# Half-size products for the values and queries of a two-layer graph network, and four moved steps in its projection stage

## The chip, the core and the metric

The kernel runs on one core of a Trainium2 chip. The metric is the device time of one execution in microseconds (us), as the median of several runs. A core has five engines, each with its own in-order queue of instructions: TensorE (in the profile PE, its weight loads PEld), VectorE (DVE), ScalarE (ACT), GpSimd (POOL) and SyncE (SP), which here only starts DMA transfers. [...]

## The reference

Two layers work on x (4096x512) and a weighted adjacency matrix adj (4096x4096), all in float32.

```python
# layer 0
h = jnp.maximum(_layernorm(x, axis=-1), 0.0)
q = h @ Wq.T + bq;  k = h @ Wk.T + bk;  v = h @ Wv.T + bv
a = q @ k.T * scale + adj + adj            # scale = 1/sqrt(512)
x = x + softmax(a, axis=-1) @ v
# layer 1: 8 heads of 64
h = jnp.maximum(_layernorm(x, axis=-1), 0.0)
nX = (h @ W).reshape(n, 8, 64).transpose(1, 0, 2)
nX = a_ln * (nX - mean) / (std + EPS) + b_ln
kg = leaky_relu(at1 + at2.transpose(0, 2, 1), 0.2) * adj    # at1, at2: nX with a1, a2
attention = softmax(where(adj != 0, kg, NEG_FILL), axis=-1)
x = x + elu(attention @ nX + nX)
```

## The kernel before, in words

`fast_path` has three stages. The projection stage (about the first 268 us) makes the values v and the queries; the attention of layer 0 follows, and from about 2100 us on the attention of layer 1. A `general_path` is taken only if a check at the end fails.

**What the projections compute.** Keys are not formed. The two weight matrices are multiplied into one, `a_sb` (Wq and Wk; four groups of matmuls, L662, copied out of PSUM by ScalarE at L666), and `queries` multiplies it with the hidden rows h; the scores are then products of these queries with h itself. `c_sb` holds what the bias bq adds. `half_scale` is half of 1/sqrt(512).

**Rounds.** The 4096 rows of x go in 8 rounds (`sb`, 0 to 7) of 512 rows, 4 tiles of 128. Each round has these parts:

- `load_x`: four DMA transfers of 256 KB on SP's queue (L548), into one of two buffers.
- `normalize`: statistics of the rows on VectorE (L172, L173), the inverse root of the variance (the power at L159 on GpSimd, the rest on VectorE, L161 to L164), then four operations on VectorE that normalize the rows (L557). It runs at the start of the round ahead of the one that uses it.
- `hidden`: 16 transposes on TensorE (L567) into two PSUM buffers, four relu operations of ScalarE (L568) that write the hidden tile `hT`, then four sums and differences of its quarters on GpSimd (L576 to L579, `hS`). Both are stored to HBM on SP's queue (L582).
- `values_of`: for each of the 4 tiles 4 matmuls of 512 columns into one PSUM buffer of four (`pv`, L588), then one addition of the bias on VectorE (L592), which writes into v.
- `queries`: for each of 4 output blocks 4 matmuls of 512 columns into the same four buffers (`pq`, L602), then one operation on VectorE (L606) that adds c_sb, multiplies by half_scale and puts the columns in another order (`sources_of_rows`) in `qs`. `qs` is stored (L610), GpSimd makes four differences of its quarters (L619 to L622), and these are stored with four transfers (L624).

The order of a round `sb` is: normalize(sb+1), load_x(sb+2), values_of(sb), hidden(sb+1), center_weights in round 2 or weigh_weights in rounds 3 to 6, queries(sb).

**Seven products.** The layer-0 attention (`stage`, L733) already multiplies the hidden rows with the queries in halves: both operands are cut into 2x2 blocks, and seven half-size products of sums of blocks (S1 to S4 and T1 to T4) stand in place of eight. That is what `hS` and the differences of the queries are for. An addition on VectorE (L741) takes each partial result out of PSUM.

**Side work.** `attention_vectors` loads small weights of layer 1 on ScalarE's queue and prepares them on VectorE (L194 to L220). `center_weights` (L230 to L232) takes the mean of each head from W on VectorE. `weigh_weights` multiplies W by the attention vectors on GpSimd (L237) and sums on VectorE (L238).

**The start.** x, Wv, then Wq and Wk in blocks (L472) are loaded on SP's queue. normalize(0), hidden(0), loads of bv and bq on ScalarE's queue (L648, L649), transposes of Wq and Wk in 32x32 blocks on VectorE (L478), values_of(0), normalize(1), attention_vectors, the products of Wq and Wk, c_sb, load_x(2), hidden(1), queries(0) follow, and then round 1.

**What sets the order.** The tile framework derives the semaphores from the data. `seq` holds instructions on each engine's queue in the order of the source, so an instruction that waits holds up all that stand behind it on its engine.

Of the kernel before, what the change touches and what calls it, by code (L numbers as in the profile page):

```python
# [78 lines left out]
def fast_path(  # L79
# [153 lines left out]

    def weigh_weights(k):
        for e in range(2):
            t = prep.tile([P, NH, HD], F32, name="prod", tag="prod", bufs=2)
            seq(nc.gpsimd.tensor_mul(t, w1_sb[:, k], aa[e]))  # L237
            seq(nc.vector.tensor_reduce(w1a_sb[:, k, e, :], t, AX.X, ALU.add))  # L238
# [223 lines left out]
    with tc.tile_pool(name="early", bufs=2) as early, tc.tile_pool(name="kv", bufs=1) as kv:  # L462
# [69 lines left out]
        with tc.tile_pool(name="proj_c", bufs=1) as pc, tc.tile_pool(  # L532
# [10 lines left out]
            bv_sb = early.tile([P, D], F32, name="bv_sb", tag="qt", bufs=16)  # L543
# [7 lines left out]
            def normalize(xt):  # L551
                mv = means(work, [xt[:, b, :] for b in range(SB)], "h")
                var = work.tile([P, SB], F32, name="hv", tag="hv", bufs=1)
                seq(nc.vector.tensor_scalar_add(var, mv[:, :, 1], LN_EPS))
                rstd = inverse_root(nc.vector, work, var, SB, "h")
                for b in range(SB):
                    seq(nc.vector.tensor_scalar(  # L557
                        xt[:, b, :], xt[:, b, :], mv[:, b, 0:1], rstd[:, b : b + 1],
                        ALU.subtract, ALU.mult,
                    ))  # L560
# [22 lines left out]

            def values_of(sb):
                for b in range(SB):
                    pv = psum.tile([P, 512], F32, name="pv", tag="mm", bufs=4)
                    for k in range(KC):
                        seq(nc.tensor.matmul(  # L588
                            pv, hidden_of[sb][0][:, k, ts(b, P)], wv_sb[k],
                            start=k == 0, stop=k == KC - 1,  # L590
                        ))
                    seq(nc.vector.tensor_add(v[:, sb * SB + b, :], pv, bv_sb))  # L592
# [3 lines left out]

            def queries(sb):
                qs = pc.tile([P, KC, GC], F32, name="qs", tag="qs", bufs=1)
                for o in range(KC):
                    pq = psum.tile([P, 512], F32, name="pq", tag="mm", bufs=4)  # L600
                    for k in range(KC):
                        seq(nc.tensor.matmul(  # L602
                            pq, a_sb[:, k, ts(o, P)], hidden_of[sb][0][:, k, :],
                            start=k == 0, stop=k == KC - 1,
                        ))
                    seq(nc.vector.tensor_scalar(  # L606
                        sources_of_rows(qs[:, o, :]), pq.rearrange("p (c q r) -> p c q r", c=SB, r=R),
                        c_sb[:, o : o + 1], half_scale, ALU.add, ALU.mult,
                    ))
# [36 lines left out]
            normalize(xts[0])  # L646
# [12 lines left out]
            for k in range(KC):  # L659
                pa_ps = psum.tile([P, 512], F32, name="pa", tag="mm", bufs=4)  # L660
# [929 lines left out]
```

## Time and profile before

| what | us |
|---|---|
| median of 3 runs | 3963.34 (3960.78 to 3963.43) |
| the profiled execution | 3960.13 |
| its span, first to last instruction | 3958.2 |
| TensorE busy in the span | 3786.1 (96%) |
| VectorE, ScalarE, GpSimd busy | 2889.7, 1796.8, 2569.7 |
| first matmul of values_of(1) to that of values_of(7) | 61.2 to 240.5 |
| last matmul of queries(7) ends, about | 268.1 |

The profile is of one execution on the chip. A row of the timeline gives a start, a duration, the engine, the line, the operation, the output and the inputs by their names, and how many instructions were merged into the row; a bracket tells the idle time of the engine before it and what ended it. [...] Each float32 matmul of the source is recorded as two instructions. A row of a line's list gives shortest, median and longest duration in nanoseconds. A wait row gives the time in total, how often, and the longest.

### The profile page before, as it was taken

The numbers are of one execution on the slowest core, as the hardware profiler recorded it, in microseconds if no ns is written. First come the engines' busy times: TensorE is split into PE (matmuls) and PEld (weight loads), VectorE is DVE, ScalarE is ACT, GpSimd is POOL, SyncE is SP. The second block draws the span as 40 slices with busy tenths as digits, with TensorE's granted clock in tenths as the row PEclk, the third lists the DMA queues.
The fourth block names the chain that finished last, engine by engine and source line by source line (L and its number), as shares of the span: only waits on it lengthen the run. The fifth ranks groups of instructions, "written<-read, shape, count | busy, mean of one in ns | idle before, by whom it ended". The sixth has DMA issues, their size and how long they took to land. (4 is left out here: it accounts for less than half of the span.)

```text
span 3958.2 us, 44075 instructions
## 1 busy us (share of the span) xinstructions
PE 3786.1 (96%) x15370; PEld 1788.6 (45%) x15370; DVE 2889.7 (73%) x4331; ACT 1796.8 (45%) x1581; POOL 2569.7 (65%) x1305
## 2 busy tenths in 40 slices
PE   8989999999999999999998899999999999999997
PEld 4446666666666666666652222222222222222222
DVE  5435556565565656556557899999999999999996
ACT  1000111111111111111115788888888888888886
POOL 3432225243242525234257999999999999999998
PEclk9999999999999999999998999999999999999999
DMA  6466657667675766768557544444444444444442
GB/s 214 169 213 195 198 175 207 199 194 213 182 220 161 223 182 191 215 183 223 164 158 190 149 141 141 145 146 138 140 138 145 140 146 146 146 139 146 129 151 79
DMA packets 554407, 670.37 MB, mean 169 GB/s; under 512 B 79808, under 2 KB 397504, under 8 KB 534720
## 3 DMA queue, kind: packets, MB, share of 16 engines
q1 hardware_dynamic: 552112, 665.70, 56.5%
q8 instruction: 122, 2.00, 0.2%
q10 hardware_dynamic: 2064, 1.77, 0.2%
q14 instruction: 109, 0.89, 0.1%
HBM read 495.12 MB, written 172.23 MB: 169 GB/s over the span
## 5 line engine op out<-in xcount | busy, mean ns | idle before, releaser
L999 POOL TENSOR_TENSOR t<-t,g 128x1536 f32<-128x1536 f32 (+1 forms) x512 | 1722.8, 3410 | 34.3 <-DVE t L992 29.1
L1015 PE MATMUL acc<-t,nX 128*64 128x512 f32 x4096 | 994.5, 606 | 66.8 <-ACT t L1002 54.5
L751 POOL TENSOR_TENSOR total<-total,aT 128x512 f32<-128x512 f32 x248 | 340.3, 1372 | 1061.3 <-ACT aT L746 1051.1
L1002 ACT ACTIVATE t<-t 128x2048 f32<-128x2048 f32 x512 | 975.9, 1906 | 85.8 <-POOL t L999 84.6
L761 PE MATMUL acc<-v,aT 128*128 128x512 f32 x2048 | 961.9, 592 | 0.0
L746 ACT ACTIVATE aT<-aT 128x512 f32<-128x512 f32 x256 | 161.2, 630 | 1322.8 <-DVE aT L741 1314.8
L992 DVE TENSOR_TENSOR t<-t,d 128x1024 f32<-128x1024 f32 x512 | 619.9, 1211 | 12.3 <-ACT t L976 12.3
L976 ACT ACTIVATE t<-d 128x1024 f32<-128x1024 f32 x512 | 524.8, 1025 | 227.7 <-PE d L969 205.0
L969 PE MATMUL d<-nb,ident_b 128*128 128x512 bf16 x2048 | 536.3, 385 | 1.5 <-DMA nb<-nT_d 1.5
L1015 PEld LDWEIGHTS acc<-t,nX 128*64 128x64 f32 x4096 | 250.4, 136 | 595.3 <-issue 340.1
L761 PEld LDWEIGHTS acc<-v,aT 128*128 128x128 f32 x2048 | 389.7, 190 | 272.4 <-issue 244.9
L986 DVE SCALAR_TENSOR_TENSOR d<-u,at2m,d 128x512 f32<-128x512 f32 x542 | 407.0, 751 | 50.1 <-PE d L969 35.2
L741 DVE TENSOR_TENSOR aT<-aT,X 128x256 f32<-128x256 f32 x512 | 214.9, 420 | 280.5 <-PE X L733 277.3
L986 DVE SCALAR_TENSOR_TENSOR t<-u,at2m,d 128x512 f32<-128x512 f32 x482 | 360.0, 747 | 49.2 <-DVE d L986 0.9
L741 DVE TENSOR_TENSOR aT<-aT,Z 128x256 f32<-128x256 f32 x384 | 159.6, 416 | 292.3 <-PE Z L733 287.6
L991 DVE TENSOR_TENSOR t<-d,g 128x512 f32<-128x512 f32 (+1 forms) x512 | 366.0, 715 | 5.1 <-DMA g<-gT_d 1.8
L725 DVE SCALAR_TENSOR_TENSOR gs<-ng,aT 128x512 f32<-128x512 bf16 x256 | 285.8, 1117 | 10.1 <-DMA gT_d<-gs 1.4
L964 PE MATMUL d<-z,z 6*128 6x512 bf16 x2048 | 250.1, 385 | 35.2 <-DVE t L991 15.4
L964 PEld LDWEIGHTS <-z 6*128 6x128 bf16 x2048 | 76.4, 91 | 443.2 <-issue 439.1
L733 PE MATMUL Z<-qt,hS 128*128 128x256 f32 x1024 | 265.7, 382 | 9.0 <-DVE aT L741 8.3
L969 PEld LDWEIGHTS <-ident_b 128*128 128x128 bf16 x2048 | 159.2, 98 | 241.6 <-issue 121.9
L733 PE MATMUL X<-qt,hS 128*128 128x256 f32 x1024 | 263.8, 380 | 0.0
(170 smaller groups left out, 3124.9 us busy)
## 6 DMA issues: line engine op xcount, KB each, us to landing
g<-gT_d SPq DMA_DIRECT2D x128, 1024.0 KB, 5.5
ag<-in_adj_dram SPq DMA_DIRECT2D x256, 256.0 KB, 5.7
hT<-h_d SPq DMA_DIRECT2D x64, 1024.0 KB, 5.9
hS<-s_d SPq DMA_DIRECT2D x64, 1024.0 KB, 8.3
gT_d<-gs SPq DMA_DIRECT2D x256, 256.0 KB, 3.0
nb<-nT_d SPq DMA_DIRECT2D x128, 512.0 KB, 5.1
nT_d<-ng SPq DMA_DIRECT2D x256, 128.0 KB, 3.4
z<-z_d SPq DMA_DIRECT2D x143, 128.0 KB, 4.7
```

Of the source, the lines that this page charges most:

```text
L733: seq(nc.tensor.matmul(out, a, b, start=start and k == 0, stop=k == 1, skip_group_check=not start,))
L741: seq(nc.vector.tensor_add(p, p, part))
L751: seq(nc.gpsimd.tensor_add(totals[ic], totals[ic], p))
L761: seq(nc.tensor.matmul(sums[ic][b], probs[s][:, ts(b, P)], v[:, jt, :], start=jt == 0, stop=jt == NB - 1))
L969: seq(nc.tensor.matmul(pair[hh // 2][:, hh % 2, :], ident_b, ng[:, jt % JB, :], start=False, stop=True))
L976: seq(nc.scalar.activation(t[:, 0:2, :], zs[n][0], AF.Relu, scale=4.0))
L986: seq(nc.vector.scalar_tensor_tensor(pair[1][:, e, :] if e > 1 - mine else t[:, 2, :], u4[:, e, :], at2m[:, jt, h : h + 1], pair[1][:, e, ...
L991: seq(nc.vector.tensor_mul(t[:, HG - mine : HG, :], pair[1][:, 2 - mine : 2, :], g))
L992: seq(nc.vector.tensor_add(t[:, 0:2, :], t[:, 0:2, :], pair[0]))
L999: seq(nc.gpsimd.tensor_mul(t[:, 0:mine, :], t[:, 0:mine, :], g))
L1002: seq(nc.scalar.activation(logits[n], logits[n], AF.Exp))
L1015: seq(nc.tensor.matmul(grp["acc"][hf][ts(e, HD), :], nX[jt // SB][:, jt % SB, hg * HG + 2 * hf + e, :], t[:, 2 * hf + e, :], start=jt == 0 ...
```

## The change

`values_of` and `queries` are computed with the seven-product scheme. A new function `seven` runs the products in four steps over two lanes; a lane is a pair of row tiles for the values, and a pair of output blocks for the queries. It has two PSUM buffers X and two Z, one of each per lane, of 256 columns. After each product, `take` moves the partial sum out on VectorE: the first into an output block adds the bias (or c_sb), the others add to what is there. Sums of blocks of Wv (`sum_wv`) and of a_sb (`sum_a`) are made once on GpSimd. half_scale goes into a_sb and c_sb. bv_sb has a buffer of its own, and `pa` has two PSUM buffers for four.

`normalize` is split. `deviations_of` makes the statistics on VectorE and the inverse root on GpSimd, with a shift, two rounds ahead; the new `normalize` applies both on ScalarE at the end of the round. `weigh_weights` keeps only GpSimd's products, and `sum_weighed` sums them on VectorE one round later. `center_weights` moves behind `queries`. A round is now: load_x(sb+2), values_of(sb), hidden(sb+1), deviations_of(sb+2), sum_weighed, queries(sb), center_weights or weigh_weights, normalize(sb+2).

```diff
@@ -231,11 +231,16 @@
         seq(nc.vector.tensor_scalar_mul(m, m, 1.0 / HD))
         seq(nc.vector.tensor_sub(w1_sb, w1_sb, m.unsqueeze(3).to_broadcast([P, KC, NH, HD])))
 
+    weighed = {}
     def weigh_weights(k):
         for e in range(2):
-            t = prep.tile([P, NH, HD], F32, name="prod", tag="prod", bufs=2)
-            seq(nc.gpsimd.tensor_mul(t, w1_sb[:, k], aa[e]))
-            seq(nc.vector.tensor_reduce(w1a_sb[:, k, e, :], t, AX.X, ALU.add))
+            weighed[k, e] = prep.tile([P, NH, HD], F32, name="prod", tag="prod", bufs=2)
+            seq(nc.gpsimd.tensor_mul(weighed[k, e], w1_sb[:, k], aa[e]))
+    def sum_weighed(k):
+        for e in range(2):
+            seq(nc.vector.tensor_reduce(w1a_sb[:, k, e, :], weighed.pop((k, e)), AX.X, ALU.add))
 
     def make_ready(ic, x1s, small, at_step, gap, last):
 
@@ -540,7 +545,12 @@
             ]
             a_sb = pc.tile([P, KC, D], F32, name="a_sb")
             c_sb = pc.tile([P, KC], F32, name="c_sb")
-            bv_sb = early.tile([P, D], F32, name="bv_sb", tag="qt", bufs=16)
+            bv_sb = pc.tile([P, D], F32, name="bv_sb")
+            wv_sums, a_sums = [
+                [early.tile([P, KC // 2, H], F32, name=name, tag="qt", bufs=16) for _ in range(4)]
+                for name in ("wvs", "as")
+            ]
 
 ...
-            def normalize(xt):
+            def deviations_of(xt):
                 mv = means(work, [xt[:, b, :] for b in range(SB)], "h")
                 var = work.tile([P, SB], F32, name="hv", tag="hv", bufs=1)
-                seq(nc.vector.tensor_scalar_add(var, mv[:, :, 1], LN_EPS))
-                rstd = inverse_root(nc.vector, work, var, SB, "h")
+                seq(nc.gpsimd.tensor_scalar_add(var, mv[:, :, 1], LN_EPS))
+                rstd = inverse_root(nc.gpsimd, work, var, SB, "h")
+                shift = work.tile([P, SB], F32, name="hs", tag="hs", bufs=2)
+                seq(nc.gpsimd.tensor_mul(shift, mv[:, :, 0], rstd))
+                seq(nc.gpsimd.tensor_scalar_mul(shift, shift, -1.0))
+                return rstd, shift
+            def normalize(xt, rstd, shift):
                 for b in range(SB):
-                    seq(nc.vector.tensor_scalar(
-                        xt[:, b, :], xt[:, b, :], mv[:, b, 0:1], rstd[:, b : b + 1],
-                        ALU.subtract, ALU.mult,
+                    seq(nc.scalar.activation(
+                        xt[:, b, :], xt[:, b, :], AF.Identity,
+                        scale=rstd[:, b : b + 1], bias=shift[:, b : b + 1],
                     ))
 
             def hidden(sb, xt):
@@ -581,32 +597,109 @@
+            def seven(product, take):
+                x, z = [
+                    [psum.tile([P, H], F32, name=name, tag=name, bufs=2) for _ in range(2)]
+                    for name in ("X", "Z")
+                ]
+                for n, todo in enumerate((
+                    ((2, z, "11", True), (1, x, "11", False)), ((5, z, "22", True), (6, x, "12", True)),
+                    ((3, z, "12", False), (7, x, "22", False)), ((4, x, "21", True),),
+                )):
+                    for lane in range(2):
+                        for which, t, _, _ in todo:
+                            product(lane, which, t[lane], which in (1, 2, 5))
+                        for _, t, block, first in todo:
+                            take(lane, block, t[lane], first)
+            def pair_product(out, a, b, start):
+                for k in range(2):
+                    seq(nc.tensor.matmul(
+                        out, a[k], b[k], start=start and k == 0, stop=k == 1,
+                        skip_group_check=not start,
+                    ))
+            SIDES = {1: ("A11", "B11"), 2: ("A12", "B21"), 3: ("S4", "B22"), 4: ("A22", "T4"),
+                     5: ("S1", "T1"), 6: ("S2", "T2"), 7: ("S3", "T3")}
+            def wv_side(name):
+                if name[0] == "T":
+                    return [wv_sums[int(name[1]) - 1][:, k, :] for k in range(2)]
+                k0, half = 2 * (int(name[1]) - 1), int(name[2]) - 1
+                return [wv_sb[k0 + k][:, ts(half, H)] for k in range(2)]
+            def sum_wv():
+                b = {f"{k + 1}{i + 1}": wv_side(f"B{k + 1}{i + 1}") for i in range(2) for k in range(2)}
+                t = [[wv_sums[e][:, k, :] for k in range(2)] for e in range(4)]
+                for out, left, right in (
+                    (t[0], b["12"], b["11"]), (t[1], b["22"], t[0]), (t[2], b["22"], b["12"]),
+                    (t[3], b["21"], t[1]),
+                ):
+                    for k in range(2):
+                        seq(nc.gpsimd.tensor_sub(out[k], left[k], right[k]))
             def values_of(sb):
-                for b in range(SB):
-                    pv = psum.tile([P, 512], F32, name="pv", tag="mm", bufs=4)
-                    for k in range(KC):
-                        seq(nc.tensor.matmul(
-                            pv, hidden_of[sb][0][:, k, ts(b, P)], wv_sb[k],
-                            start=k == 0, stop=k == KC - 1,
-                        ))
-                    seq(nc.vector.tensor_add(v[:, sb * SB + b, :], pv, bv_sb))
+                def product(pair, which, out, start):
+                    a, b = SIDES[which]
+                    pair_product(out, side_a(sb, pair, a), wv_side(b), start)
+                def take(pair, block, part, first):
+                    half = ts(int(block[1]) - 1, H)
+                    to = v[:, sb * SB + 2 * pair + int(block[0]) - 1, half]
+                    seq(nc.vector.tensor_add(to, part, bv_sb[:, half] if first else to))
+                seven(product, take)
 
 
             half_scale = 0.5 / math.sqrt(D)
+            def a_side(name, o):
+                if name[0] == "S":
+                    return [a_sums[int(name[1]) - 1][:, k, ts(o, P)] for k in range(2)]
+                k0, half = 2 * (int(name[2]) - 1), int(name[1]) - 1
+                return [a_sb[:, k0 + k, half * H + o * P : half * H + (o + 1) * P] for k in range(2)]
+            def sum_a():
+                a = {f"{i + 1}{k + 1}": a_sb[:, 2 * k : 2 * k + 2, ts(i, H)]
+                     for i in range(2) for k in range(2)}
+                seq(nc.gpsimd.tensor_sub(a_sums[0], a["22"], a["21"]))
+                seq(nc.gpsimd.tensor_add(a_sums[1], a_sums[0], a["11"]))
+                seq(nc.gpsimd.tensor_sub(a_sums[2], a["21"], a["11"]))
+                seq(nc.gpsimd.tensor_sub(a_sums[3], a["12"], a_sums[1]))
+            def rows_side(sb, name):
+                h, sums = hidden_of[sb]
+                if name[0] == "T":
+                    return [sums[:, (2, 1, 0, 3)[int(name[1]) - 1], k] for k in range(2)]
+                h = h.rearrange("p k (t j r) -> p k j t r", j=2, r=P)
+                return [h[:, 2 * (int(name[1]) - 1) + k, int(name[2]) - 1] for k in range(2)]
 
             def queries(sb):
                 qs = pc.tile([P, KC, GC], F32, name="qs", tag="qs", bufs=1)
-                for o in range(KC):
-                    pq = psum.tile([P, 512], F32, name="pq", tag="mm", bufs=4)
-                    for k in range(KC):
-                        seq(nc.tensor.matmul(
-                            pq, a_sb[:, k, ts(o, P)], hidden_of[sb][0][:, k, :],
-                            start=k == 0, stop=k == KC - 1,
-                        ))
-                    seq(nc.vector.tensor_scalar(
-                        sources_of_rows(qs[:, o, :]), pq.rearrange("p (c q r) -> p c q r", c=SB, r=R),
-                        c_sb[:, o : o + 1], half_scale, ALU.add, ALU.mult,
-                    ))
+                def product(o, which, out, start):
+                    a, b = SIDES[which]
+                    pair_product(
+                        out.rearrange("p (t r) -> p t r", r=P), a_side(a, o), rows_side(sb, b), start
+                    )
+                def take(o, block, part, first):
+                    o = 2 * (int(block[0]) - 1) + o
+                    to = qs[:, o, :].rearrange("p (q t j r) -> p j t q r", q=SB, j=2, r=R)
+                    to = to[:, int(block[1]) - 1]
+                    part = part.rearrange("p (t q r) -> p t q r", q=SB, r=R)
+                    if first:
+                        seq(nc.vector.tensor_scalar_add(to, part, c_sb[:, o : o + 1]))
+                    else:
+                        seq(nc.vector.tensor_add(to, part, to))
+                seven(product, take)
 ...
             load_blocks(raw["k"], wkT)
             xts[1] = load_x(1)
             seq(nc.sync.dma_start(out=wk_rows, in_=wkT.rearrange("(k p) o -> p k o", p=P)))
-            normalize(xts[0])
+            of_next = deviations_of(xts[0])
+            sum_wv()
+            normalize(xts[0], *of_next)
             hidden(0, xts.pop(0))
             seq(nc.scalar.dma_start(out=bv_sb, in_=bv[None, :].to_broadcast([P, D])))
             seq(nc.scalar.dma_start(out=bq_sb, in_=bq[None, :].to_broadcast([P, D])))
             for name in ("q", "k"):
                 for c in range(SB):
                     turn_blocks(turned[name][:, c, :], raw[name], c)
+            of_next = deviations_of(xts[1])
             values_of(0)
-            normalize(xts[1])
+            normalize(xts[1], *of_next)
             attention_vectors(v[:, 15, :])
             seq(nc.gpsimd.tensor_mul(
                 wk_rows, wk_rows, bq_sb.unsqueeze(1).to_broadcast([P, KC, D])
             ))
             for k in range(KC):
-                pa_ps = psum.tile([P, 512], F32, name="pa", tag="mm", bufs=4)
+                pa_ps = psum.tile([P, 512], F32, name="pa", tag="mm", bufs=2)
                 for c in range(SB):
                     seq(nc.tensor.matmul(
                         pa_ps, turned["q"][:, c, ts(k, P)], turned["k"][:, c, :],
                         start=c == 0, stop=c == SB - 1,
                     ))
-                seq(nc.scalar.copy(a_sb[:, k, :], pa_ps))
+                seq(nc.scalar.mul(a_sb[:, k, :], pa_ps, half_scale))
             seq(nc.vector.tensor_reduce(c_sb, wk_rows, AX.X, ALU.add))
+            seq(nc.vector.tensor_scalar_mul(c_sb, c_sb, half_scale))
+            sum_a()
             xts[2] = load_x(2)
             hidden(1, xts[1])
+            of_next = deviations_of(xts[2])
             queries(0)
+            normalize(xts[2], *of_next)
             for sb in range(1, NS):
-                if sb + 1 < NS:
-                    normalize(xts[sb + 1])
 ...
                 values_of(sb)
                 if sb + 1 < NS:
                     hidden(sb + 1, xts[sb + 1])
+                if sb + 2 < NS:
+                    of_next = deviations_of(xts[sb + 2])
+                if 4 <= sb < 4 + KC:
+                    sum_weighed(sb - 4)
+                queries(sb)
                 if sb == 2:
                     center_weights()
-                elif 3 <= sb < 3 + KC:
+                if 3 <= sb < 3 + KC:
                     weigh_weights(sb - 3)
-                queries(sb)
+                if sb + 2 < NS:
+                    normalize(xts[sb + 2], *of_next)
```

More of the change, by code (lines that the diff above doesn't have):

```diff
@@ L689, in fast_path @@
                     hidden(sb + 1, xts[sb + 1])
+                if sb + 2 < NS:
[3 more added lines that the diff above has]
+                queries(sb)
                 if sb == 2:
                     center_weights()
-                elif 3 <= sb < 3 + KC:
+                if 3 <= sb < 3 + KC:
                     weigh_weights(sb - 3)
-                queries(sb)
+                if sb + 2 < NS:
+                    normalize(xts[sb + 2], *of_next)
+            assert not weighed
         with tc.tile_pool(name="attn", bufs=2) as work, tc.tile_pool(
```

## The prediction

> **What bounds the kernel now.** I read the stretches of 20 us first, because the change touches only the projections, the first seventh of the run, and because a mean over 3958 us says nothing of them. The columns are the stretch, its length, then the busy time (and instructions) of PE, weight loads, VectorE, ScalarE and GpSimd, the granted clock, the DMA share and GB/s.
>
> ```profile
> 120.00:140.00 20.00, 19.61 (x58) 9.46 (x57) 9.61 (x22) 2.17 (x4) 6.65 (x6) 1.00 0.52 185
> 140.00:160.00 20.00, 20.00 (x48) 8.87 (x47) 10.92 (x24) 0.00 (x0) 11.51 (x10) 1.00 0.56 204
> 260.00:280.00 20.00, 12.85 (x34) 6.88 (x33) 7.06 (x13) 0.00 (x0) 4.97 (x4) 0.88 0.50 169
> ```
>
> TensorE fills the rounds; VectorE and GpSimd are half free, DMA too. So here a saved TensorE microsecond is a saved microsecond of the end, as long as nothing else gets in the way. The third row is the hand-over to attention.
>
> Next the timeline (start, duration, engine, line, and in brackets idle time before and who ended it): one round, then the start.
>
> ```profile
> 120.99 13.90 PE L588 MATMUL pv<-wv_sb,hT 128*128 128x512 f32 x32
> 137.13 13.90 PE L602 MATMUL pq<-hT,a_sb 128*128 128x512 f32 x32
> ...
> 14.59 14.53 PE L588 MATMUL pv<-wv_sb,hT 128*128 128x512 f32 x32
> ...
> 28.22 2.49 DVE L478 STREAM_TRANSPOSE v<-v 128x512 f32<-128x512 f32 x4 [9.66 <-DMA v<-in_wkT_dram]
> 30.64 2.45 DVE L592 TENSOR_TENSOR v<-pv,bv_sb 128x512 f32<-128x512 f32 x4
> 31.34 14.00 PE L662 MATMUL pa<-v 128*128 128x512 f32 x32 [2.23 <-DVE v L592]
> ```
>
> A values or queries product is 32 TensorE instructions (16 in the source, each recorded twice) in 13.73 us (120.99 to the transposes at 134.72), 429 ns apiece. The start is another matter: VectorE runs its queue in order, so the 4 bias additions of values(0) sit behind the transposes of k, which wait for a load until 28.2. Four PSUM buffers let TensorE finish values(0) without them; it loses 2.2 us.
>
> **The products.** Half-size operands with seven products already exist in attention, and there I take the price:
>
> ```profile
> 1002.29 1.03 PE L733 MATMUL X<-qt,hT 128*128 128x256 f32 x4
> 1003.15 1.02 PE L761 MATMUL acc<-v,aT 128*128 128x512 f32 x2
> ...
> L741 DVE TENSOR_TENSOR aT<-aT,X x512: 397/421/423, 277.3 to 2068.6; 128x256 f32<-128x256 f32 x171
> ```
>
> One half-size pair product, 4 instructions, takes 0.86 us start to start (215 ns apiece). A call makes 7 products in 2 lanes: 14 x 0.86 = 12.04 us against 13.73, so 1.69 us less. [...] there are now 56 for 32. Unoverlapped, at the 190 ns that the trace gives a load of 128x128 f32, a call would go from 32 x (190 + 429) = 19.8 us to 56 x (190 + 215) = 22.7, and 16 calls would lose 46 us. The trace disagrees: 190 ns loads lie inside a 215 ns pitch at L733, and inside 429 at L588. I follow the row. Loads still fit, with 25 ns to spare.
>
> 15 of the 16 calls lie in the packed rounds (values(0) is in the start): 15 x 1.69 = **25.4 us saved**.
>
> **VectorE's price in a round.** A call had 4 evictions of 0.68 to 0.75; it now has 14 half-size additions of 0.42 (row above; strided ones of the queries perhaps 0.45), 5.9 to 6.3 us in 12.0. Normalizing (4 x 0.54) leaves VectorE, statistics stay (4 x 0.79 = 3.2). A round gives 12.2 + 3.2, sometimes 1.4 for weight sums (2 x 0.69), under 17 of about 26.5 us. What matters is the hand-over, since only two X and two Z buffers exist, one per lane. Within a lane a buffer is needed again 1.7 to 2.6 us after its product ends, and x of lane 1 in the last step 0.86 after; an addition starts 0.2 after the matmul and takes 0.42. In attention, with a single Z, all Z products together waited 9.0 us for VectorE, most of it the 8.3 around 277 and 290. I take nothing for it. The statistics now stand ahead of the queries' additions: from the end of the values' matmuls, 0.6 for the last addition, 3.2 (or 4.6 with sums), so they end 3.9 to 5.3 later. The transposes take 2.4 and the first reuse of Z comes 3.4 after that, at 5.8: covered, with 0.1 to spare in rounds 4 and 5. The loads of x that they need are issued about 6 to 8 us into the round, behind the four t_d stores on SP's queue, and land in 4.5: at 13, against need at 12.6 to 15. Covered by 1 to 2 us, no more.
>
> **Where the cover is gone: the centering of the weights.** It moves from before to after queries(2) on VectorE. Now (105.66 to 111.55) it is 2.28 + 0.18 + 3.36 us:
>
> ```profile
> 105.66 2.28 DVE L230 TENSOR_REDUCE w1m<-w_sb 128x32 f32<-128x2048 f32 x1
> 108.19 3.36 DVE L232 TENSOR_TENSOR w_sb<-w_sb,w1m 128x2048 f32<-128x2048 f32 x1
> 109.47 3.20 POOL L577 TENSOR_TENSOR hS<-hS,hT 128x512 f32<-128x512 f32 x1
> ```
>
> Behind it stand the additions of values(3). TensorE does 4 products (3.4 us), then wants Z back; VectorE is free at 0.6 + 5.9 + about 0.7 = 7.2 and gives it at 7.7. **Cost 4.3 us**. The 0.7 is because GpSimd's subtractions for the queries run then: in the third row L577 takes 3.2 instead of 1.27 while L232 holds it up. Ends: 3.4 without contention, 6 with twice as much.
>
> **GpSimd, ScalarE, SP.** GpSimd gets 8 small operations per round (0.23, 1.02 for the power, six of 0.20 to 0.24; with gaps 3.2 us, by L258 to L262 in attention), between the hidden sums and the queries' subtractions: 5.1 + 3.2 + 5.1 + 2.5 of 26.5. ScalarE gets 4 x 0.80 (L268), and is idle 85%. Both have 10 us before anyone needs them. SP's queue keeps its order. sum_a (4 x 1.27 on GpSimd) follows the last a_sb copy; its first result is ready 2 us after the pa products, needed 5.8 after. Each costs nothing.
>
> **The start** is where the change gives back. Statistics end at 7.5; then 3.2 on GpSimd (was 2.1 on VectorE) and 3.2 of ScalarE (was 1.9): hidden(0) ends at 17.0 instead of 14.6. values(0) runs 4 products, to about 20.5, and stops: its additions stand on VectorE behind the transposes of k and now also behind xts[1]'s statistics. What decides is when wk and x land:
>
> ```profile
> SPq L472 <- DMA bv_sb<-in_bv_dram: 4.6, 1, 4.6
> ...
> 277.26 2.08 PE L733 MATMUL Z<-qt,hS 128*128 128x256 f32 x4 [6.31 <-DVE aT L741]
> ```
>
> The first row is SP's wait: wk's second load went out at 19.71, as bv's (issued by ScalarE at 14.84, 4.9 us) landed; the third and fourth fit the landings of bq and a1T, x's second that of a2T. Two ends. Waits as now, all 2.4 later: k turned at 33.1, statistics 36.4, TensorE goes on at 36.9. Waits gone, because a1T, a2T and the two small ones now leave ScalarE only after xts[1]'s normalization: wk streams behind wq at the 185 GB/s of 10 to 15 us, lands near 20, k is turned at 22.5, x lands near 26, statistics end near 28, TensorE goes on at 28.4. I take the second, since four of the six loads are moved away and the moved wait is the named one. Then 10 products, 8.6 us, and the clock: after 6.3 us idle, four matmuls took 2.08 (row above) and full speed was back 4.8 us later, which cost 2.4. 28.4 + 8.6 + 2.4 = 39.4; the pa products, 13.84, to 53.2. Now they end at 45.2: **8.0 us lost** (16.5 at the other end, 6 if x lands with wk). Behind it the attention vectors (8 to 9 us on VectorE), c_sb (2.3) and statistics (3.2) end near 57, needed at 58.4; covered.
>
> **Sum**: -25.4 + 8.0 + 4.3 + 0.5 (a chance in four of a cold clock, 2 us, after the stall of 4.3: the trace shows 6.3 us idle to be enough and 2.2 not) - 0.3 (the last eviction, 0.42 for 0.75) + 0.5 for takes of 0.45 and the thin covers = -12.4 us. The hand-over at 269 to 277, which waits for the q_d store (4.2 us) and VectorE, keeps its length. The profiled execution took 3960.1 (span 3958.2 and 1.9 around), so 3947.7 for it; the median of the three runs is 3.2 higher: **3951**.
>
> **Rivals.** (1) *The start keeps its waits*: 8.5 us more lost, gain 3.9, 3959. For it: bv still leaves ScalarE early, only later. Chance 0.18. (2) *Slower, by the buffers*: if giving a buffer back to TensorE costs s in each of the 8 lane-steps of the 16 calls, the sum turns at s = 12.4/128 = 0.10 us; at 0.2 it is 13 slower, 3976. For it: one buffer per lane where there were four, a margin of 0.1 to 0.2 in the last step. Against: attention does the same without loss. 0.09. (3) *x lands late*: the loads come 3 us after my estimate, and the queries' additions wait behind statistics; past 1.5 us of slack, 1.5 us in each of 5 rounds, 3958. 0.10. (4) *The saving isn't there*, TensorE's pitch being 240 ns with weights in the way: 56 x 25 ns x 16 = 22 us back, 3973. 0.03. (5) *Better start*: TensorE is held only until 24 and the centering costs 3.4: 3945. 0.10. The forecast itself has 0.50, own range 3947 to 3955.4.
>
> 0.2% is 7.9 us, about what a measurement of this kernel can tell from no change. Forecast and (5) are faster, with a fifth of (3) and some of (1): 0.66. (1) and (3) otherwise are no change: 0.22. (2) and (4): 0.12. For 8 in 10 the range takes in (5) and (1): 3945 to 3961.
>
> **What would show it.** Right: half-size matmuls at 215 ns in stretches of 12.0 us, rounds of about 26.5 us, one gap of some 4 us in values(3) ended by VectorE, a gap of about 8 us near 20 to 28 ended by it too, pa ending near 53, attention starting near 257. Wrong: gaps before Z or X in every round, VectorE waiting for x of its statistics, or the values(0) gap lasting to 37.

## The result, and the profile after

The changed kernel takes 3949.77 us (median of 9 executions, 3947.56 to 3954.27) where the kernel before takes 3962.93 (9 executions, 3960.75 to 3963.55): a ratio of 0.9967, 95% interval 0.9959 to 0.9976, 13.2 us less. The forecast was 3951. The profiled execution took 3951.69 with a span of 3949.9.

An ordinary stretch of 20 us of the kernel after (length, then busy time and instructions of PE, weight loads, VectorE, ScalarE and GpSimd, granted clock, DMA share, GB/s):

```profile
140.00:160.00 20.00, 20.00 (x97) 17.66 (x98) 11.59 (x28) 4.32 (x7) 14.92 (x18) 1.00 0.54 205
```

TensorE stays full although it now has 97 matmuls for 48, and the 17.66 us of weight loads (0.18 us each) lie beside them.

The timeline of TensorE in the kernel after (start, duration, engine, line, output and inputs, merged instructions; in brackets idle time before and who ended it). L618 is the half-size product, L758 the products of Wq and Wk, L838 attention. X and Z are the PSUM tiles that these products write and VectorE's additions read (L653, `v<-Z,bv_sb`):

```profile
29.79 2.04 PE L618 MATMUL Z<-wvs,hS 128*128 128x256 f32 x4 [7.94 <-POOL hv L564]
...
39.98 13.90 PE L758 MATMUL pa<-v 128*128 128x512 f32 x32
53.72 1.04 PE L583 MATMUL pt<-ident,xt 128*128 128x128 f32 x8
...
68.13 1.03 PE L618 MATMUL Z<-wv_sb,hT 128*128 128x256 f32 x4
...
80.21 1.04 PE L583 MATMUL pt<-ident,xt 128*128 128x128 f32 x8
...
128.18 1.87 PE L618 MATMUL Z<-wvs,hS 128*128 128x256 f32 x4 [3.55 <-DVE v L653]
129.84 1.91 PE L618 MATMUL X<-wvs,hS 128*128 128x256 f32 x4
131.55 1.15 PE L618 MATMUL Z<-wvs,hS 128*128 128x256 f32 x4
...
257.18 1.13 PE L838 MATMUL Z<-qt,hT 128*128 128x256 f32 x4 [0.58 <-DVE qs L698]
```

A row lasts past the start of the next (129.84 and 1.91 make 131.75, the next begins at 131.55), so costs are taken from start to start. A call goes from 68.13 to 80.21: 12.08 us, 216 ns for each of its 56 instructions. There are two holes, near 21.7 to 29.8 and near 124.6 to 128.2. Attention's first product starts at 257.18 (before at 268.96), and the gap behind it is as long as it was (6.31). The list of TensorE's waits from the start to 260 us has nothing else above 2 us, apart from the wait for the first rows of x (12.8):

```profile
PE Z L618 <- POOL hv L564: 7.9, 1, 7.9
PE Z L618 <- DVE v L653: 3.5, 1, 3.5
```

The name in the first row misleads. VectorE's timeline shows who really held TensorE at the start (L483 turns a block of Wk, L172 and L173 are the statistics of the second block of x, L653 the first addition of values(0)):

```profile
22.73 2.49 DVE L483 STREAM_TRANSPOSE v<-v 128x512 f32<-128x512 f32 x4 [3.34 <-DMA v<-in_wkT_dram]
25.14 0.65 DVE L172 BATCH_NORM_STATS2 hst<-xt 128x6 f32<-128x512 f32 x1
...
28.43 0.69 DVE L172 BATCH_NORM_STATS2 hst<-xt 128x6 f32<-128x512 f32 x1 [0.27 <-DMA xt<-in_x_dram]
29.25 0.39 DVE L653 TENSOR_TENSOR v<-Z,bv_sb 128x256 f32<-128x256 f32 x1
...
124.40 3.29 DVE L232 TENSOR_TENSOR w_sb<-w_sb,w1m 128x2048 f32<-128x2048 f32 x1
127.62 0.41 DVE L653 TENSOR_TENSOR v<-Z,bv_sb 128x256 f32<-128x256 f32 x1
```

The addition that frees Z starts at 29.25, right behind the statistics, and TensorE resumes at 29.79, half a microsecond later. At 127.62 the same happens behind the centering.

**Where the time went**, from the two traces. In the kernel before, the products of Wq and Wk end and attention starts here:

```profile
45.18 1.04 PE L567 MATMUL pt<-ident,xt 128*128 128x128 f32 x8
268.96 1.13 PE L733 MATMUL Z<-qt,hT 128*128 128x256 f32 x4 [0.84 <-DVE qs L606]
```

The stage up to attention's first product became 11.8 us shorter. The rest of the run took 3689.2 us before (3958.2 - 268.96) and 3692.7 after (3949.9 - 257.18), so the profiled execution shows 8.3 us at its end. Of the 3.5 us, 0.8 have come in by the boundary of the layers, most of it in the first 30 us: a stretch of half clock at 278.6, which the trace before does not have (the last section shows the steps ahead of both), less a shorter slow restart behind the gap of 6.31 (at half clock for 2.8 us from the restart, before for 4.8). The other 2.7 come in at the boundary, from about 2070 to 2110, half of them as slow matmuls (half clock lasts 27.3 us there for 23.9), half as longer waits; why is left open. In the traces of the experiments below the same rest took 3687.8 to 3691.8 us, in no order that goes with their projections.

### The profile page after: what moved, and what is told of

Its sections match the earlier page's. It is cut to its first block, busy times and chain, and to the rows that moved or that the text cites. A ratio compares the mean times of both kernels' runs of the same rounds, so it can differ in the third digit from the quotient of the medians.

```text
span 3949.9 us, 45153 instructions
## 1 busy us (share of the span) xinstructions
PE 3767.2 (95%) x15754; PEld 1862.5 (47%) x15754; DVE 2912.2 (74%) x4420; ACT 1820.1 (46%) x1613; POOL 2589.2 (66%) x1373
## 5 line engine op out<-in xcount | busy, mean ns | idle before, releaser
L838 PE MATMUL Z<-qt,hS 128*128 128x256 f32 x1024 | 264.9, 381 | 8.9 <-DVE aT L846 8.3
L838 PE MATMUL X<-qt,hS 128*128 128x256 f32 x1024 | 264.2, 381 | 0.0
```

The source lines that it names most:

```text
L838: seq(nc.tensor.matmul(out, a, b, start=start and k == 0, stop=k == 1, skip_group_check=not start,))
```

## The experiments

The kernel before was run again beside each group of them, and the ratios go by those runs. Their medians lie between 3962.5 and 3964.7, so a difference of two medians from different groups is uncertain by about 2 us.

### The seven products without the moves

```diff
-            of_next = deviations_of(xts[1])
             values_of(0)
-            normalize(xts[1], *of_next)
+            normalize(xts[1])
...
             for sb in range(1, NS):
+                if sb + 1 < NS:
+                    normalize(xts[sb + 1])
...
-                if sb + 2 < NS:
-                    of_next = deviations_of(xts[sb + 2])
-                if 4 <= sb < 4 + KC:
-                    sum_weighed(sb - 4)
+                if sb == 2:
+                    center_weights()
+                elif 3 <= sb < 3 + KC:
+                    weigh_weights(sb - 3)
+                    sum_weighed(sb - 3)
                 queries(sb)
```

`normalize` is that of the kernel before, with all its operations on VectorE but the power.

> The seven products and their sums stay; the three moves are undone (statistics and normalization on VectorE at the start of the round, centering and weight sums ahead of the queries). My theory: the moves are what makes the products pay, because two X and two Z buffers give TensorE only 3.4 us before it needs VectorE. In rounds 1 to 6 normalization (3.2 statistics, a power that waits on GpSimd behind the queries' subtractions, 1.9 for four operations) ends about 9.6 us into the round: a stall of some 6.6 us and a cold clock, 6 x 8 = 50. The weight sums wait for GpSimd's products: some 6 us and a cold clock in rounds 3 to 6, 4 x 8 = 32. Start about 10 lost, products 24.7 gained: 4030, between 4000 and 4045. Rival: the moves only tidy, and the products alone bring the same or more: 3940 to 3952.

Measured: 4051.21 us (4050.43 to 4054.88), ratio 1.0220, 95% interval 1.0204 to 1.0235 (before there 3964.68). TensorE's waits to 372 us:

```profile
PE Z L612 <- DVE v L647: 44.1, 7, 12.5
PE Z L612 <- DVE qs L692: 32.8, 5, 9.2
```

TensorE waits for VectorE in 12 of the 16 calls. Attention starts at 359.0, 101.8 us later than in the kernel after: TensorE is idle for 71.6 us more, and busy for 30.3 us more with the same instructions (260.77 us for 230.51), because one stretch of half clock goes with each of the twelve waits, 88.7 us in all. The theory holds in kind. The size was missed by 21 us and lies outside its own range. The waits in the rounds are the 64 us expected (76.9 less the 12.5 at the start, against 6 x 6.6 + 4 x 6); but the start lost 19.4 us (`pa` ends at 64.57 for 45.18) where 10 were taken, since Wk was turned only at 36.6, and half clock cost the rounds more than the 16 taken for it. So the buffers do become the bound when VectorE has something long ahead of the additions. The mechanism of the rival "slower, by the buffers" is real; the moved steps keep it away.

### The moves without the seven products

```diff
             def values_of(sb):
...
-                seven(product, take)
+                for b in range(SB):
+                    pv = psum.tile([P, 512], F32, name="pv", tag="mm", bufs=4)
+                    for k in range(KC):
+                        seq(nc.tensor.matmul(
...
+                    seq(nc.vector.tensor_add(v[:, sb * SB + b, :], pv, bv_sb))
```

The queries go back to 512 columns in the same way, `pa` has its four buffers again, and the sums of blocks are gone.

> The 512-column products with four PSUM buffers stay as before; only the moves are made (statistics two rounds ahead, inverse root on GpSimd, normalization on ScalarE, centering behind the queries, sums a round later). My theory: rounds stay bound by TensorE at 29.9 us, four buffers cover everything, the start is even: 3963, within 3 us of before. Rival: freeing VectorE is itself worth something: below 3955.

Measured: 3960.70 us (3958.06 to 3966.11), ratio 0.9990, interval 0.9983 to 0.9996. In TensorE's timeline:

```profile
30.23 13.90 PE L744 MATMUL pa<-v 128*128 128x512 f32 x32
```

The products of Wq and Wk begin 1.1 us earlier than before (31.34), and no round has a wait. The time is within the expected 3 us. With four buffers neither hole exists, so the holes at the start and at the centering are costs of the moved order together with the two X and two Z buffers. From this kernel to the kernel after attention starts 9.7 us earlier (257.18 for 266.92): the 24.8 of the products less 9.8 at the start (`pa` at 39.98 for 30.23) and 5.3 at the centering.

### The start: which end of the estimate, and why

The four small loads of layer 1 (a1T, a2T, a_ln, b_ln) go out on ScalarE's queue right behind bq, as they did before, in the kernel after:

```diff
             seq(nc.scalar.dma_start(out=bq_sb, in_=bq[None, :].to_broadcast([P, D])))
+            load_vectors()
...
-    def attention_vectors(prod):
+    def load_vectors():
         for t, a in ((aa[0], a1T), (aa[1], a2T)):
             seq(nc.scalar.dma_start(
```

> Changed kernel, but the four loads of layer 1's small vectors leave ScalarE right behind bq's, as they did before the change, instead of behind the normalization of the second block. My theory of the start: wk's blocks and x's second block then go out behind these loads again, k is turned only near 31 to 33 us instead of 25.2, and TensorE resumes values(0) near 35 to 37 instead of 29.8: 5 to 7 us slower than the changed kernel, 3956. Rival: the loads of wk come early for another reason, and nothing moves: 3950.

Measured: 3957.85 us (3954.22 to 3962.47), ratio 0.9983, interval 0.9975 to 0.9992: 8.1 above the kernel after, and its attention starts 8.0 later (265.21). TensorE, then VectorE:

```profile
36.70 2.05 PE L620 MATMUL Z<-wvs,hS 128*128 128x256 f32 x4 [15.68 <-POOL hv L566]
```

```profile
30.58 2.49 DVE L485 STREAM_TRANSPOSE v<-v 128x512 f32<-128x512 f32 x4 [13.38 <-DMA v<-in_wkT_dram]
```

TensorE resumes at 36.70 (the forecast's other end: 36.9) and the products of Wq and Wk end at 61.75, 16.6 us later than before (other end: 16.5). The opposite edit, in the kernel before, delays the four loads until behind the first copy of a_sb:

```diff
-            attention_vectors(v[:, 15, :])
             for k in range(KC):
...
                 seq(nc.scalar.copy(a_sb[:, k, :], pa_ps))
+                if k == 0:
+                    load_vectors()
+            attention_vectors(v[:, 15, :])
```

> The kernel before, with only the four small vector loads moved on ScalarE's queue behind the first copy of the weight products. My theory, that these loads hold up wk's blocks: wk lands near 22 instead of 28.2, k is turned near 25, values(0) runs through on its four buffers and the weight products begin at 29.1 instead of 31.3: 2.2 us less. Rival: wk is held up by something else, and k is turned at 28.2 to 30.7 as before: no change.

Measured: 3957.64 us (3955.38 to 3959.01), ratio 0.9988, interval 0.9981 to 0.9995 (before there 3962.54).

```profile
28.03 13.90 PE L663 MATMUL pa<-v 128*128 128x512 f32 x32
```

Wk was turned at 21.08 for 28.22 and the 2.2 us of idle time ahead of `pa` are gone. Attention starts 3.4 us earlier (265.55); the median is 4.9 lower where 2.2 were expected, and what goes beyond 3.4 lies behind the projections or is scatter.

Both kernels agree: with the four loads at the early place in the program, Wk's come 7 to 8 us later. How, the issues of the loads show. First the kernel after, then the one with the early loads (issue rows, then SP's waits):

```profile
10.14 4.89 SPq L477 DMA_DIRECT2D v<-in_wkT_dram  x4
17.39 0.39 ACTq L743 DMA_DIRECT2D bv_sb<-in_bv_dram  x1
SPq L558 <- DMA bv_sb<-in_bv_dram: 7.5, 1, 7.5
```

```profile
13.62 7.78 SPq L479 DMA_DIRECT2D v<-in_wkT_dram  x4
17.67 0.44 ACTq L194 DMA_DIRECT2D a_sb<-in_a1T_dram  x1
SPq L479 <- DMA v<-in_wqT_dram: 6.3, 1, 6.3
SPq L479 <- DMA bv_sb<-in_bv_dram: 6.1, 1, 6.1
```

It is not the traffic of the four: Wk's first load is already late at 13.62, and they are issued from 17.67 on. The records of the loads in the traces name semaphores. Eight of them (101 to 108) serve the loads of both queues in turn, and most records state a wait on the load's own semaphore. Where the queue is held up, a load goes out as the load that had the number before has landed: in the kernel before Wk's second at 19.71 (104, bv's landed at 19.70), in the kernel after the second one of x's second block at 23.78 (104, bv's landed at 23.76). In the kernel after Wk's loads have 107, 108, 101 and 102, used before by loads of Wv and Wq, and all are out by 15.03, ahead of bv's. With the early loads they have 103 to 106: the first waits for Wq's to land, the second for bv's. In the kernel after it is the second block of x that waits for bv, for 7.5 us. Why the place of the four loads changes these numbers is not shown.

### The start without its hole

```diff
             seq(nc.sync.dma_start(out=wk_rows, in_=wkT.rearrange("(k p) o -> p k o", p=P)))
+            load_vectors()
...
             for name in ("q", "k"):
                 for c in range(SB):
                     turn_blocks(turned[name][:, c, :], raw[name], c)
-            of_next = deviations_of(xts[1])
             values_of(0)
+            of_next = deviations_of(xts[1])
             normalize(xts[1], *of_next)
```

`load_vectors` starts the four small loads on SP's queue here. The statistics of the second block stand behind the additions of values(0); the turns of Wk stay ahead.

> Changed kernel, with the statistics of the second block behind the additions of values(0) instead of ahead of them, and the four small vector loads on SP's queue behind wk's rows, so that they don't wait for these statistics. My theory: TensorE's stop in values(0) ends when VectorE reaches its additions. With the statistics out of the way that is when k is turned, near 25.2: TensorE resumes at about 25.7 instead of 29.8 and comes back warmer, so the products of the two weight matrices end 4 to 6 us earlier (48 to 50 instead of 53.7): 3944 to 3946. Rival: the landing of x or the vector loads is what counts, and the stop or a new one in queries(0) takes the gain back: 3949 or more.

Measured: 3951.82 us (3946.69 to 3953.21), ratio 0.9969, interval 0.9958 to 0.9980: no gain over the kernel after, where 3944 to 3946 were expected. TensorE, then ScalarE:

```profile
24.08 1.10 PE L620 MATMUL Z<-wvs,hS 128*128 128x256 f32 x4 [2.53 <-DVE v L655]
34.48 7.03 PE L761 MATMUL pa<-v 128*128 128x512 f32 x16
46.68 9.71 PE L761 MATMUL pa<-v 128*128 128x512 f32 x15 [5.18 <-ACT a_sb L765]
```

```profile
43.22 2.93 ACT L575 ACTIVATE xt<-xt,hs,hr 128x512 f32<-128x512 f32 x4 [25.33 <-POOL hs L570]
46.05 1.05 ACT L765 ACTIVATE a_sb<-pa 128x512 f32<-128x512 f32 x2
```

The hole shrank to 2.53 us and `pa` began 5.5 us earlier. But ScalarE's queue has the normalization of the second block ahead of the copies of `pa`, and it waits for GpSimd until 43.22; `pa` has two PSUM buffers and stops. It ends at 56.66, 2.9 later than in the kernel after. One mended wait had become another. The next kernel moves only the normalization:

```diff
-            normalize(xts[1], *of_next)
             for k in range(KC):
...
                 seq(nc.scalar.mul(a_sb[:, k, :], pa_ps, half_scale))
+                if k == 2:
+                    normalize(xts[1], *of_next)
```

> The start of e3_start, with the four normalizations of xts[1] on ScalarE behind the third a_sb copy and no longer ahead of the first. Theory: what stopped the pa products there was the order of ScalarE's queue alone, so pa now runs unbroken, 34.5 to about 48.2 (e3_start: 34.5 to 56.7; the kernel after: 40.0 to 53.7), and the transposes of hidden(1) follow without a stop: 5.5 us less than the kernel after, so about 3945 (3943 to 3947). Rival: the a_sb copies were late for another reason, or the transposes now wait for the normalization: a stop of 3 us or more stays before or behind pa, and the time is 3948 or more.

Measured: 3944.58 us (3942.93 to 3947.25), ratio 0.9953, interval 0.9939 to 0.9966 (before there 3963.96).

```profile
34.70 13.90 PE L760 MATMUL pa<-v 128*128 128x512 f32 x32
```

`pa` runs unbroken and ends at 48.4, 5.3 us ahead of the kernel after; the time is 5.2 lower. The order of ScalarE's queue alone was the cause. A wait of 1.3 us for the sums of hidden(1) on GpSimd is left.

### The centering in pieces

```diff
-                if sb == 2:
-                    center_weights()
+                if 2 <= sb < 2 + KC:
+                    center_weights(sb - 2)
```

Each call centers a quarter of W.

> Changed kernel, with the centering cut into four pieces of some 1.5 us, one behind the queries in each of rounds 2 to 5. My theory: the gap in values(3) (3.7 us of stall and 1.6 of cold clock at 124 to 132 us) is all the centering's, and a piece of 1.5 us fits in the 3.4 us of cover: both go away, 5.3 us less, 3944.5. Rival: GpSimd's subtractions, which run at the same time, hold the pieces up, and four small gaps take the place of the one: 3948 to 3951.

Measured: 3946.91 us (3945.53 to 3949.62), ratio 0.9954, interval 0.9941 to 0.9968: 2.9 less than the kernel after (4.6 if each is compared with the kernel before of its own group), 5.3 expected. TensorE's waits, then the last two of the three operations of one piece on VectorE:

```profile
PE Z L620 <- DVE v L655: 2.9, 4, 0.7
```

```profile
124.41 0.80 DVE L233 TENSOR_SCALAR w1m<-w1m 128x8 f32<-128x8 f32 x1
125.24 1.71 DVE L234 TENSOR_TENSOR w_sb<-w_sb,w1m 128x512 f32<-128x512 f32 x1
```

The hole and its stretch of half clock are gone, but four holes of 0.7 us came instead, as the rival said. A piece takes 3.2 us (0.68, 0.80 and 1.71) and not the 1.5 expected, since GpSimd's subtractions of the queries run at that moment (see the last section). In this execution the start was 2.1 us longer, because TensorE resumed 0.7 later (30.47) and half clock lasted one step of 3.4 us more; from the end of `pa` to attention it takes 201.84 us for 203.46. So the gain of this edit is 1.6 us by the profile and 2.9 to 4.6 by the medians, and which part is chance is not shown.

### All of it

Side work on VectorE goes between the additions: each addition of `seven` may be followed by one small operation from a list. The attention vectors go behind values(1)'s additions, the centering into round 3's, Wk's turns into values(0)'s; the statistics stand behind values(0); the small loads go on SP's queue.

```diff
                         for _, t, block, first in todo:
                             take(lane, block, t[lane], first)
+                            if fill:
+                                fill.pop(0)()
```

> Changed kernel with all of VectorE's side work of the projections put between the additions, one small operation behind each: the turns of k behind every third addition of values(0), the attention vectors from values(1) on, the centering in twelve pieces in values(3); statistics of the second block behind values(0), vector loads on SP's queue. My theory: an addition every 0.86 us leaves 0.44 us of VectorE free, and a buffer is wanted again 1.7 us or more after its product, so operations up to 0.9 us fit. TensorE stops in values(0) only for the landing of bv (near 22), the weight products begin near 31.5 instead of 40, the gap in values(3) is gone: 8.5 + 5.3 = 14 us less than the changed kernel, 3936. Rival: the fine cover is used up and TensorE waits a little at many additions: 3945 or more.

Measured: 3941.13 us (3938.93 to 3942.72), ratio 0.9942, interval 0.9929 to 0.9956: 5 us short of the expectation. Its trace has the stop in `pa` again (3.45 us, for the copy of a_sb), and one of 2.0 in values(0), for bv, whose addition starts at 22.31. So three more places were changed: the normalization as above, bv's load ahead of everything, Wk's turns behind the 8th, 10th, 12th and 14th addition.

> e5_best with three places mended: the same order on ScalarE, bv's load issued ahead of everything else, and the four turns of wk's blocks behind the 8th, 10th, 12th and 14th addition. Theory: each stop that e5_best still shows costs its length: 2.0 us for bv with 1.6 of low clock behind it, and 3.5 inside pa. pa begins near 30 (e5_best: 33.3) and ends unbroken near 44, and the time is about 3933 (3931 to 3936). Rival: bv's quarter megabyte ahead of x and the later turns of wk only move the stops (pa begins at 32 or later), or the gain is lost to a longer stretch of low clock later: 3938 or more.

Measured: **3933.63 us** (3933.18 to 3934.32), ratio 0.9924, interval 0.9911 to 0.9938, faster than both kernels. TensorE:

```profile
31.73 13.90 PE L774 MATMUL pa<-v 128*128 128x512 f32 x32
```

The time is as expected, and before attention no wait for an addition and no stretch of half clock is left. `pa` begins at 31.7 and not near 30: with bv ahead of it, the first rows of x reach TensorE 1 us later (13.1 for 12.1). Attention starts at 243.8, 13.4 us before that of the kernel after.

## Why the prediction was right

The forecast was 3951 with a sum of -12.4; 3949.8 came, -13.2. Its terms against the two traces:

| term | forecast | measured |
|---|---|---|
| products, 15 calls | -25.4 | -24.8 (15 x (13.73 - 12.08)) |
| transposes, 6 rounds | 0 | -0.8 (2.27 for 2.41) |
| the start, end of `pa` | +8.0 | +8.5 (53.72 for 45.18) |
| centering, with the cold clock | +4.3, +0.5 | +3.7, +1.6 |
| covers, last eviction, rest | +0.2 | 0.0 (what is left) |
| stage | -12.4 | -11.8 |

**The products.** The forecast's 215 ns came as 216, and the weight loads fit inside it: 98 of them, 17.66 us in all, lie within 20 us of matmuls. The forecast's other case, loads that do not overlap, was 22.7 us a call; a call takes 12.08. The row of attention decided rightly. What lets the loads overlap is not shown.

**The start.** Of its two ends the forecast chose that the waits go, because four of six loads leave ScalarE later. Both ends were then run: TensorE resumes at 29.8 as the kernel stands (forecast 28.4), and at 36.7 with the loads early (36.9). The kernel before with late loads shows the same from the other side. The reason given is right only in part: the waits of Wk's loads did go because the four loads stand later, but not by their traffic, and bv's landing, the wait that the forecast named, was handed on to x. TensorE resumes 1.4 later than forecast because Wk is there only at 22.7 (near 20 in the forecast, which took 185 GB/s for 10 to 15 us, where the mean of that stretch is 155) and the last rows of x at 28.4 (near 26), behind that wait. The clock makes part of it good: 0.8 less was lost to it.

**The centering.** The hole is 0.6 us shorter than forecast: L231 and L232 took 0.44 and 3.29 (before 0.18 and 3.36), where 0.7 was added for GpSimd's subtractions beside them. The cold clock was taken as a chance of one in four worth 2 us; it came, and cost 1.6 (two products in 3.37 us for 1.73). As an estimate from the counts of the last section, it was likelier than that: wherever the borders lie, a stop of 4.3 us leaves at least 2.15 us idle in one step of 3.41, so at most 1.26 busy, and a slow step followed in all 35 cases of 1.44 or less. So the cold clock was rightly named and its term was 1.1 us too small, the two together 0.5.

**The buffers.** Nothing was taken for the hand-back, with break-even at 0.10 us per lane-step. In the rounds the trace shows no wait for an addition except the centering's, so the rival "slower" had no part in the result. The experiment without the moves shows that this hangs on what stands ahead of the additions on VectorE: there the same buffers cost 77 us of waits. "x lands late" did not come in the rounds, and the pitch of 240 ns, an assumption of the author's, not at all (216). "The start keeps its waits" (3959) is the experiment with early loads, 3957.9.

**What was not foreseen** is that the profiled execution gives 3.5 us of the stage's gain back behind it and the median does not. The rest of the run differs from trace to trace by up to 4.9 us. That the median agrees with the sum to 0.8 us is therefore in part luck; what the traces confirm is the sum for the stage, -11.8 for -12.4.

## What to carry to other kernels

When products are cut smaller and their buffers halved, price the products from a row, then look for each long operation that stands ahead of an eviction on the same engine's queue: at the start and at the centering such operations gave back 13.8 of 25.6 us, and with all left in place they turned the gain into a loss of 87. Small operations put between the evictions left no wait for an addition in the last kernel, where the centering in one block cost a hole of 3.7 us and 1.6 of slow clock after it. Where a wait is mended, follow the next engine's queue as well: ScalarE's order took back all that the first mended start had won.

## What the runs showed of the hardware

**The clock.** In the clock records of these traces half clock comes in steps of 3.41 us that lie on one grid. In the kernel after its stretches begin at 25.97, 128.37, 261.49 and 278.56, which lie 30, 39 and 5 steps of 3.413 us apart; every other trace has such a grid. Slow steps went with little busy TensorE in the step before, as the counts below the rows say; what sets the clock is not shown. The rows have the columns of the ordinary stretch shown under the result (third from the end is the granted clock); two are of the kernel before, two of e5_best:

```profile
29.50:32.92 3.42, 1.58 (x4) 0.86 (x5) 3.42 (x7) 0.00 (x0) 0.00 (x0) 1.00 1.07 409
32.92:36.33 3.41, 3.41 (x9) 1.50 (x9) 3.24 (x10) 0.58 (x1) 0.00 (x0) 1.00 1.00 422
20.01:23.43 3.42, 1.38 (x7) 0.91 (x6) 1.02 (x3) 0.00 (x0) 2.62 (x3) 1.00 0.55 189
23.43:26.84 3.41, 3.41 (x10) 2.66 (x9) 2.13 (x6) 0.00 (x0) 0.00 (x0) 0.50 0.87 273
```

A stop of 2.23 us (29.11 to 31.34) is cut by the border at 29.50 and leaves 1.58 us busy: no slow step follows. A stop of 2.04 us (20.84 to 22.88) lies in one step and leaves 1.38: the next is slow, though TensorE is at work again. In all eleven traces, from the first step at full clock to the end of attention in layer 0, a step at full clock with 1.44 us or less of busy TensorE was followed by a slow one each time (35 of 35), one with more than 1.48 never; between these both occur. A slow step was followed by another when TensorE was busy for at most 2.81 us in it (35 of 35), and by none from 2.84 on (40 of 40). A stop of 1.96 us behind attention's first products fell into one step in the kernel after (275.15 to 278.56, 1.45 busy) and had a slow stretch behind it; in the kernel before a border at 288.92 cut the same stop (2.94 and 1.93 busy), and it had none.

**VectorE beside GpSimd.** The same two operations of the centering in the last kernel, the first piece while GpSimd subtracts, the second when it has ended:

```profile
114.94 1.26 POOL L725 TENSOR_TENSOR ts<-qs 128x512 f32<-128x512 f32 x1
115.22 1.01 DVE L243 TENSOR_SCALAR w1m<-w1m 128x8 f32<-128x8 f32 x1
116.16 1.27 POOL L726 TENSOR_TENSOR ts<-qs,ts 128x512 f32<-128x512 f32 x1
116.47 1.50 DVE L243 TENSOR_TENSOR w_sb<-w_sb,w1m 128x512 f32<-128x512 f32 x1
...
119.16 0.15 DVE L243 TENSOR_SCALAR w1m<-w1m 128x8 f32<-128x8 f32 x1
119.56 0.68 DVE L243 TENSOR_TENSOR w_sb<-w_sb,w1m 128x512 f32<-128x512 f32 x1
```

An operation on 8 elements takes 1.01 for 0.15, and ends at 116.23 just as GpSimd's does (116.20); one on 512 takes 1.50 for 0.68. GpSimd's stay at 1.26 to 1.27 here, but in the kernel before L577 took 3.20 beside L232, for a median of 1.26. The additions out of PSUM took 0.41 or 0.42 in either case here, and 0.39 to 0.43 in all calls of values in the kernel after. There 14 of them per call in place of 4 fit beside GpSimd's work, which takes 14.92 us of the ordinary 20.
